# When a scatter is let go: threes of chunks, then quarters of a step, and a head in another order

## The chip, the cores and the metric

The kernel runs on one core of a Trainium2 chip. Its engines are TensorE (PE, with its weight loads shown apart as PEld), VectorE (DVE), ScalarE (ACT), GpSimd (POOL) and SyncE (SP); each works through its own instruction list in order, and they wait for each other through semaphores. The metric is the time of one execution on the device, in microseconds; shorter is better. The kernel before took 5031.5 us (median of 3 runs, 5031.15 to 5031.81).

## The reference

One layer of a graph network: 12,500 nodes with 128 features, 412,500 edges with 20 features, sorted by destination. `src` says to which node an edge's message is added, `dst` from which node it is taken.

```python
def ssp(x):
    return jax.nn.softplus(x) - LOG2
h = x @ W_in2f                              # here x is relu(layernorm(x))
Wij = ssp(f_ij @ W_f1 + b_f1) @ W_f2 + b_f2
Wij = Wij * rcut_ij[:, None]
x_ij = h[idx_j] * Wij                       # idx_j = dst
agg = jax.ops.segment_sum(x_ij, idx_i, num_segments=h.shape[0])   # idx_i = src
out = ssp(agg @ W_o1 + b_o1) @ W_o2 + b_o2
...
return x + out
```

## The kernel before

**Tiling.** The edges go in 806 chunks of 512 (`CH`), each of four tiles of 128 (`QT`). Four chunks make a group, whose inputs (f, rcut, window offsets) are loaded together. The nodes stand in 98 blocks of 128 and are prepared by quads of four blocks (`make_h`: layer norm, ReLU, product with W_in2f, split into bf16 parts, store to DRAM in the tables h, h_1, h_2, h_3). Quad 0 is `h[0]`, quad 1 is `h[1]`, and a third list, `aside`, makes the others from step 7 on.

**A chunk's way.** PE computes `z = f @ W_f1` for two chunks at a time (`hidden`, L710); ACT and DVE make the softplus of it (L719, L720, L722 and L742); PE computes the filter `v` (`value`, L834). Since the edges are sorted by destination, a chunk's gathered nodes lie in a window of 42 rows: SP loads it (`near`, L656), DVE builds a one-hot matrix (`window`, L818), PE picks the rows out (`pick`, L846), and ACT multiplies them by rcut (`picked`, hg, L856). DVE multiplies v by hg: that is the message `o` (L864).

**The sum by source.** Messages are not added at once. A counting sort on the fly gives each edge a slot: DVE compares block numbers (`blocks`, inb, L747), two PE matmuls add up the counts (`pass_on`, L799, and `rank`, L766; called "the counts" below), and DVE reads the rank out (`rank_end`, top, L771). POOL then writes the chunk's messages into slot tables in DRAM, with one indirect DMA per tile, so four scatters a chunk (`scatter`, L873). The slot tables belong to seven segments of chunks (`SEGS`: the first has 88 groups, chunks 0 to 351). When a segment is written, a `Collect` loads its slots back (m), compares (L932) and adds with matmuls (`add`, L953: acc and numbers). The first collect begins at chunk 352 + 17 = 369 (`DELAY` = 17). So the program has a stage A, chunks up to 368 without collects, and a stage B with them. In the end the output MLP and the residual follow.

**What sets the order.** The program's order is written out by hand: `step(k)` issues, for each engine, the work that belongs to step k, which is for PE v of chunk k+1, the pick of chunk k+2, the counts of a chunk some six ahead, z, and in stage B the collect's matmuls; each engine runs its instructions in that order. In the head, `HEAD = (0, 2, 4)` names steps with a special order.

**Pacing.** There are 16 message buffers (`BACK`). `behind` makes PE's v, pick and z of a chunk wait for scatters 16 chunks back (14 to 16 in effect). A scatter itself waits for the message (DVE), for the landing of the scatter eight before it (eight semaphores in turn), and, from chunk 24 (`PACED`) to the last twelve chunks, for PE: `scatter(k, kept["v"])`, called in `step(k)` right behind v of chunk k+1, lets chunk k-1 go, and its first scatter waits for that v. The other three follow it on POOL in order.

```python
if j >= PACED and k < NCH - PACED // 2   # else: no wait for PE
```

Of the kernel before, what the change touches and what calls it, by code (L numbers as in the profile page):

```python
# [17 lines left out]
P = 128  # L18
# [3 lines left out]
QT = CH // P  # L22
# [23 lines left out]
def gnn_kernel(  # L46
# [20 lines left out]
    nc = tc.nc  # L67
# [477 lines left out]
    with tc.tile_pool(name="edge", bufs=2) as edge, tc.tile_pool(  # L545
# [49 lines left out]
        def behind(inst, k, i):  # L595

            if k - BACK >= 0:
                tc.add_manual_dep(inst.ins, puts[(k - BACK) * QT + i],
                                  mybir.DependencyInfo(mybir.DependencyClass.Sync,
                                                       mybir.DependencyReason.DATA),  # L600
                                  reason="pace of the scatters")

        class Group:
# [101 lines left out]
            def hidden(self, c):  # L705

                z = psum.tile([P, 2, CH], F32, name="z")
                for k in range(2):
                    rows = slice(32 * (c + k), 32 * (c + k) + RBF)
                    mm = nc.tensor.matmul(z[:, k, :], wf1[rows, :], self.f[rows, :],  # L710
                                          start=True, stop=True)
                    if k == 1:
                        behind(mm, self.g * NCHUNK + c - LZ, 3)
                self.pair[c] = z

            def hidden_log(self, c):
# [36 lines left out]
            def rank(self, c):  # L753

                seg = self.seg
                if c == 0:
                    self.top = edge.tile([P, TG], F32, name="top")
                    self.slot = edge.tile([P, TG], I32, name="slot", bufs=8)
                k = self.g * NCHUNK + c
                if k > seg.c0:  # L760
                    self.pass_on()
                if k == seg.cleared and k > seg.c0:
                    used = self.used()
                    self.limit(6 * len(segs), ALU.is_gt, seg.low, used[:, :, :NBLK - 1])
                    self.limit(6 * len(segs) + 1, ALU.is_gt, seg.low_last, used[:, :, NBLK - 1:])
                nc.tensor.matmul(free, after, self.inb[c], start=k == seg.c0, stop=False,  # L766
                                 skip_group_check=True)
                kept["inb"] = self.inb[c]

            def rank_end(self, c):  # L770
# [58 lines left out]
            def value(self, c, v):  # L829

                r = self.pair[c // 2 * 2][:, c % 2, :]
                k = self.g * NCHUNK + c - 1
                for i in range(QT):
                    mm = nc.tensor.matmul(v[:, i, :], r[:, i * P:(i + 1) * P], wf2,  # L834
                                          start=False, stop=True, skip_group_check=True)
                    if i == 1:
                        behind(mm, k, k % 2)
                kept["v"] = mm
                return v

            def pick(self, c, at, ps):

                near = self.near.pop(c)
                k = self.g * NCHUNK + c - 2
                for i in range(QT):
                    mm = nc.tensor.matmul(ps[:, i, :], at[:, i * P:(i + 1) * P], near,  # L846
                                          start=i == 0, stop=i == QT - 1, skip_group_check=True)
                    if i == 1:
                        behind(mm, k, 2 + k % 2)

            def picked(self, c, ps):

# [11 lines left out]
                nc.vector.tensor_mul(o[:, :, :P], v, hg)  # L864
                self.o[c] = o

            def scatter(self, c, after=None):

                views = self.seg.views
                o = self.o.pop(c)  # L870
                for i in range(QT):
                    j = c * QT + i
                    put = nc.gpsimd.indirect_dma_start(  # L873
                        out=views[j % VIEWS],
                        out_offset=bass.IndirectOffsetOnAxis(ap=self.slot[:, j:j + 1], axis=0),
                        in_=o[:, i, :],
                        in_offset=None,
                    )
                    puts.append(put.ins.name)
                    if i == 0 and after is not None:  # L880
                        tc.add_manual_dep(
                            put.ins, after.ins.name,
                            mybir.DependencyInfo(mybir.DependencyClass.Sync,
                                                 mybir.DependencyReason.DATA),
                            reason="pace of TensorE")
                    if i == 0 and self.g * NCHUNK + c == self.seg.cleared:
                        for name in self.seg.clears:
                            tc.add_manual_dep(
                                put.ins, name,
                                mybir.DependencyInfo(mybir.DependencyClass.Sync,  # L890
                                                     mybir.DependencyReason.DATA),
                                reason="cleared slots")

        class Collect:
# [47 lines left out]
            def add(self, u):  # L942
                b0, nb, t0, nt = self.units[u]
                m, to = self.m.pop(u), self.to.pop(u)
                for j in range(nb * nt):
                    b, t = b0 + j // nt, t0 + j % nt
                    if b % QT == 0 and t == 0:
                        self.few = QT if "rest" in kept else 2
                    few = self.few
                    i = b % few  # L950
                    if i == 0 and t == 0:
                        self.acc[b // few] = self.room(b // few)
                    nc.tensor.matmul(self.acc[b // few][:, i, :], m[:, j, :P], to[:, j, :],  # L953
                                     start=t == 0, stop=t == self.seg.tiles(b) - 1)
# [42 lines left out]
        def of(k):  # L997
            return groups[k // NCHUNK], k % NCHUNK
# [14 lines left out]
        def pairs(make):  # L1013
            return lambda g, c: None if c % 2 else make(g, c)
# [34 lines left out]
        tops, ps = [], {}  # L1049
        waiting = []  # L1050
        LAG, PACED = 1, 24

        def step(k, units=()):

# [11 lines left out]
            def message(k):  # L1066
                g, c = of(k)
                g.message(c, vs.pop(k), hgs.pop(k))
                waiting.append(k)
                scatter(k)  # L1070

            def scatter(k, after=None):
                while waiting and (waiting[0] < PACED or k >= NCH - PACED // 2
                                   or after is not None and waiting[0] <= k - LAG):
                    j = waiting.pop(0)
                    g, c = of(j)
                    g.scatter(c, after if j >= PACED and k < NCH - PACED // 2 else None)

            if k in vs:
                message(k)  # L1080
            if not k:
                next(h[1])
            for r in tops:
                for _ in r:
                    pass
# [41 lines left out]
            for r in ready[-1:]:  # L1127
                next(r, None)
                tops.append(r)
            if k in HEAD:  # L1130
                part("end", made["log"] - 1, pairs(hidden_end))
            elif k != -1:
                part("log", min(k + LZ - 1, made["hidden"]), pairs(hidden_log))
            if k not in HEAD[:-1]:
                part("hidden", k + LZ, pairs(hidden))
            for c, u in units:
                if summed:
                    summed[0].add(summed[1])
                summed[:] = c, u

        zeros = {}
        units = {}
# [129 lines left out]
        with tc.manual_schedule():  # L1272
# [36 lines left out]
            for k in range(-3, max(NCH, max(units) + 1)):  # L1309
# [140 lines left out]
```

## Time and profile before

| | |
|---|---|
| median of 3 runs | 5031.5 us (5031.15 to 5031.81) |
| profiled execution, its own time | 5066.4 us |
| its span, first to last instruction | 5064.7 us |
| mean granted TensorE clock | 0.784 |
| instructions | 68,387 |
| scatters (L873) | 3224, mean 959 ns |
| moved by DMA | 858 MB, mean 169 GB/s |

The profile comes from one execution, which took 0.7% longer than the median. Busy times are by engine, in microseconds; a busy PE is not PE at its peak. The granted clock is the share of full speed that the chip gave TensorE. In a row of groups the last column is the idle time of the engine just before those instructions and what ended most of it: "issue" means that nothing in the profile was waited for, "remote" that a semaphore was waited for of which the profile shows no setter. In a row of a timeline the idle time before the instruction stands in brackets.

### The profile page before, as it was taken

How to read it: one execution, taken by the hardware profiler on the slowest of the kernel's cores; microseconds unless marked ns; L12 is line 12 of the kernel's file. 1: busy time of each engine (PE TensorE's matmuls, PEld its weight loads, DVE VectorE, ACT ScalarE, POOL GpSimd, SP SyncE). 2: the span in 40 equal slices, each digit the busy share in tenths (PEclk: the TensorE clock that was granted, in tenths of full speed). 3: DMA queues.
4: the chain of work that ended last, by engine and by line, in shares of the span. 5: the costliest groups of instructions: out<-in, count | busy, mean ns of one | idle time of the engine just before them, and what ended most of it. 6: DMA issues, size and time to landing. Idle time of an engine off the chain costs nothing. (4 is left out here: it accounts for less than half of the span.)

```text
span 5064.7 us, 68387 instructions
## 1 busy us (share of the span) xinstructions
PE 3601.4 (71%) x21594; PEld 2760.7 (55%) x21594; DVE 3149.0 (62%) x7192; ACT 2793.9 (55%) x5494; POOL 3135.5 (62%) x3298
## 2 busy tenths in 40 slices
PE   5666666566655565567777887887777787787778
PEld 3444444344433344356666666666666666666667
DVE  5565555555544454556666666666666676677767
ACT  5556566565555555555555555555555555555533
POOL 5566666666666666666666666666656666666553
PEclk7666666766666666679999888888988888888889
DMA  4555545445433334446657655567656765665658
GB/s 140 171 160 164 171 138 174 147 134 160 130 99 114 113 113 141 131 154 199 190 189 238 187 178 185 175 192 230 188 169 185 219 207 168 183 216 163 186 144 229
DMA packets 494767, 858.10 MB, mean 169 GB/s; under 512 B 141018, under 2 KB 276558, under 8 KB 494398
## 3 DMA queue, kind: packets, MB, share of 16 engines
q1 hardware_dynamic: 390798, 640.38, 42.3%
q0 software_dynamic: 103168, 213.15, 12.5%
q8 instruction: 174, 2.85, 0.2%
q14 instruction: 195, 1.60, 0.1%
q10 hardware_dynamic: 432, 0.13, 0.0%
HBM read 457.62 MB, written 395.69 MB: 168 GB/s over the span
## 5 line engine op out<-in xcount | busy, mean ns | idle before, releaser
L873 POOL DMA_INDIRECT slots<-o,slot x3224 | 3090.8, 959 | 1831.2 <-issue 808.9
L856 ACT ACTIVATE hg<-picked,rcut 128x128 f32<-128x128 f32 x3224 | 913.3, 366 | 1243.5 <-remote 356.7
L834 PEld LDWEIGHTS v<-wf,r 128*128 128x128 f32 x6448 | 1067.2, 247 | 324.2 <-issue 214.8
L834 PE MATMUL v<-wf,r 128*128 128x128 f32 x6448 | 1153.8, 335 | 73.4 <-issue 36.5
L864 DVE TENSOR_TENSOR o<-v,hg 128x512 f32<-128x512 f32 x806 | 553.0, 686 | 698.4 <-remote 207.0
L953 PEld LDWEIGHTS acc<-to,m 128*128 128x128 f32 x5660 | 782.1, 219 | 281.0 <-issue 144.0
L953 PE MATMUL acc<-to,m 128*128 128x128 f32 x5660 | 836.6, 308 | 117.1 <-DVE agg L987 45.2
L710 PE MATMUL z<-f,wf 20*128 20x512 f32 x1612 | 605.7, 826 | 355.7 <-issue 185.6
L771 DVE TENSOR_REDUCE top<-free 128x4 f32<-128x392 f32 x806 | 449.1, 557 | 602.2 <-remote 341.9
L932 DVE TENSOR_TENSOR to<-numbers,m 128x640 f32<-128x640 f32 (+3 forms) x793 | 630.4, 825 | 40.0 <-remote 12.0
L719 ACT ACTIVATE a<-z,bf 128x1024 f32<-128x1024 f32 x402 | 445.7, 1109 | 379.4 <-PE v L834 113.6
L747 DVE TENSOR_TENSOR inb<-numbers,blk 128x392 f16<-128x392 f32 x806 | 447.7, 556 | 297.3 <-PE picked L846 73.9
L846 PE MATMUL picked<-near,at 126*128 126x128 bf16 x3224 | 393.6, 248 | 330.2 <-issue 193.5
L799 PE MATMUL free<-inb,rest_of 128*128 128x392 f16 x806 | 318.1, 395 | 420.9 <-issue 277.2
L742 DVE SCALAR_TENSOR_TENSOR r<-z,nbf,a 128x1024 f32<-128x1024 f32 x402 | 513.5, 1277 | 127.9 <-ACT a L722 64.0
L826 ACT ACTIVATE v<-bf 128x512 f32<-128x512 f32 x806 | 486.6, 604 | 180.7 <-DVE o L864 72.5
L846 PEld LDWEIGHTS <-at 126*128 126x128 bf16 x3224 | 302.7, 114 | 389.7 <-issue 364.5
L953 PE MATMUL numbers<-to,m 128*128 128x128 f32 x2492 | 398.7, 324 | 121.0 <-DVE to L932 87.6
L953 PEld LDWEIGHTS numbers<-to,m 128*128 128x128 f32 x2492 | 367.5, 233 | 213.6 <-DVE to L932 136.6
L722 ACT ACTIVATE a<-a,half 128x1024 f32<-128x1024 f32 x402 | 461.5, 1148 | 13.1
L710 PEld LDWEIGHTS z<-f,wf 20*128 20x128 f32 x1612 | 152.4, 226 | 551.7 <-issue 303.0
L720 ACT ACTIVATE a<-a 128x1024 f32<-128x1024 f32 x402 | 424.9, 1057 | 12.8
(126 smaller groups left out, 1845.0 us busy)
## 6 DMA issues: line engine op xcount, KB each, us to landing
m<-slots SPq DMA_DIRECT2D x307, 387.0 KB
rel<-rel_d SPq DMA_DIRECT2D x202, 504.0 KB
m<-slots SPq DMA_DIRECT2D x278, 322.5 KB
f<-in_f_t SPq DMA_DIRECT2D x101, 512.0 KB
slots<-o,slot POOLq DMA_INDIRECT x3224
m<-slots SPq DMA_DIRECT2D x193, 258.0 KB
slots<-zero SPq DMA_DIRECT2D x96, 387.0 KB
slots<-zero SPq DMA_DIRECT2D x58, 516.0 KB
```

The lines of the kernel that those rows point to most:

```text
L710: mm = nc.tensor.matmul(z[:, k, :], wf1[rows, :], self.f[rows, :], start=True, stop=True)
L722: nc.scalar.activation(a, a, AF.Ln, bias=half, scale=0.5)
L742: nc.vector.scalar_tensor_tensor(r, z, nbf1, a, op0=ALU.max, op1=ALU.add)
L771: nc.vector.tensor_reduce(self.top[:, c * QT:(c + 1) * QT], free_v, axis=mybir.AxisListType.X, op=ALU.max)
L826: nc.scalar.activation(v, spread(bf12, QT), AF.Copy)
L834: mm = nc.tensor.matmul(v[:, i, :], r[:, i * P:(i + 1) * P], wf2, start=False, stop=True, skip_group_check=True)
L846: mm = nc.tensor.matmul(ps[:, i, :], at[:, i * P:(i + 1) * P], near, start=i == 0, stop=i == QT - 1, skip_group_check=True)
L856: nc.scalar.activation(hg[:, i, :], ps[:, i, :], AF.Copy, scale=self.rcut[:, j:j + 1])
L864: nc.vector.tensor_mul(o[:, :, :P], v, hg)
L873: put = nc.gpsimd.indirect_dma_start(out=views[j % VIEWS], out_offset=bass.IndirectOffsetOnAxis(ap=self.slot[:, j:j + 1], axis=0), in_=o[: ...
L932: nc.vector.tensor_tensor(to[:, :n, :], count_ps[:, None, :].to_broadcast([P, n, P]), m[:, :n, P:].to_broadcast([P, n, P]), op=ALU.is_equal)
L953: nc.tensor.matmul(self.acc[b // few][:, i, :], m[:, j, :P], to[:, j, :], start=t == 0, stop=t == self.seg.tiles(b) - 1)
```

## The change

Three parts.

1. `kept["mm"]` now holds the last matmul that was issued by any of z, counts, v, pick or the collect's add (before: `kept["v"]`, v alone). `scatter(k, point)` is called at four points of a step: behind v, behind the pick, behind the counts, and at the end. For chunks 24 to 368 it lets go twelve scatters (three chunks) at once, at the point "v", and only the first of the twelve waits for PE. From chunk 369 on (`LONE`) it lets go one scatter at each of the four points, and each waits for the last matmul issued there. Chunks under 24 and the last twelve steps are not paced, as before.
2. Quad 1 of the nodes, `h[1]`, was moved on in every step from 0 (in step 0 twice); now it begins in step 6.
3. In steps 1 and 3, z and v of the odd chunk k+2 are issued right behind the pick, ahead of the counts. Step 4 too now makes the next chunk's message early (`k <= HEAD[-1]`).

```diff
...
-                kept["v"] = mm
+                kept["mm"] = mm
...
                 nc.vector.tensor_mul(o[:, :, :P], v, hg)
                 self.o[c] = o
 
-            def scatter(self, c, after=None):
+            def scatter(self, c, tiles, after=None):
 
                 views = self.seg.views
-                o = self.o.pop(c)
-                for i in range(QT):
+                o = self.o[c] if tiles[-1] < QT - 1 else self.o.pop(c)
+                for i in tiles:
                     j = c * QT + i
                     put = nc.gpsimd.indirect_dma_start(
                         out=views[j % VIEWS],
...
                         in_offset=None,
                     )
                     puts.append(put.ins.name)
-                    if i == 0 and after is not None:
+                    if i == tiles[0] and after is not None:
                         tc.add_manual_dep(
                             put.ins, after.ins.name,
                             mybir.DependencyInfo(mybir.DependencyClass.Sync,
...
         tops, ps = [], {}
         waiting = []
         LAG, PACED = 1, 24
+        LONE = segs[0].c1 + DELAY
 
         def step(k, units=()):
 
...
             def message(k):
                 g, c = of(k)
                 g.message(c, vs.pop(k), hgs.pop(k))
-                waiting.append(k)
+                waiting.append((k, 0))
                 scatter(k)
 
-            def scatter(k, after=None):
-                while waiting and (waiting[0] < PACED or k >= NCH - PACED // 2
-                                   or after is not None and waiting[0] <= k - LAG):
-                    j = waiting.pop(0)
-                    g, c = of(j)
-                    g.scatter(c, after if j >= PACED and k < NCH - PACED // 2 else None)
+            def scatter(k, point=None):
+                while waiting:
+                    j, i = waiting[0]
+                    if j < PACED or k >= NCH - PACED // 2:
+                        n, after = QT - i, None
+                    else:
+                        where, n = ("v", 3 * QT) if j < LONE else ("each", 1)
+                        if point not in (("v", "pick", "rank", "end") if where == "each" else (where,)):
+                            return
+                        if j * QT + i + n > (k - LAG + 1) * QT:
+                            return
+                        after = kept["mm"]
+                    while n > 0:
+                        j, i = waiting.pop(0)
+                        g, c = of(j)
+                        e = min(QT, i + n)
+                        g.scatter(c, range(i, e), after)
+                        after = None
+                        n -= e - i
+                    if e < QT:
+                        waiting.insert(0, (j, e))
+                        return
 
             if k in vs:
                 message(k)
-            if not k:
-                next(h[1])
             for r in tops:
                 for _ in r:
                     pass
...
                 hgs[k + 1] = g.picked(c, ps.pop(k + 1))
                 if k + 1 not in vs:
                     vs[k + 1] = g.value(c, bs.pop(k + 1))
-                    scatter(k, kept["v"])
+                    scatter(k, "v")
             if k in HEAD:
                 part("log", k + LZ - 1, pairs(hidden_log))
             if has(k + 2):
...
                 if k + 2 not in ps:
                     ps[k + 2] = psum.tile([P, QT, P], F32, name="picked", tag="v", bufs=3)
                 g.pick(c, ats.pop(k + 2), ps[k + 2])
+                scatter(k, "pick")
                 if k + 2 > 0:
                     bs[k + 2] = g.bias(c)
+                if k in (1, 3):
+                    part("hidden", k + LZ, pairs(hidden))
+                    vs[k + 2] = g.value(c, bs.pop(k + 2))
             part("window", k + 3, window)
             if k not in HEAD:
                 part("end", min(k + LZ - 2, made.get("log", -1)), pairs(hidden_end))
...
                     keep()
             if k < NCH:
                 keep()
-            if 0 <= k < HEAD[-1]:
+            if 0 <= k <= HEAD[-1]:
                 message(k + 1)
             upto = max(made["rank"], min(k + LR, 2 * k + 3))
             ready = [ranks(j) for j in range(made["rank"] + 1, upto + 1)]
...
             for r in ready[-1:]:
                 next(r, None)
                 tops.append(r)
+            scatter(k, "rank")
             if k in HEAD:
                 part("end", made["log"] - 1, pairs(hidden_end))
             elif k != -1:
...
                 if summed:
                     summed[0].add(summed[1])
                 summed[:] = c, u
+            scatter(k, "end")
 
         zeros = {}
         units = {}
...
                 step(k, now)
 
                 if k >= 0:
-                    for m in h:
+                    for m in h[:1] if k <= HEAD[-1] + 1 else h:
                         next(m, None)
                 if k > NEXT - 3:
                     next(aside, None)
```

In stage A, POOL's list at chunk 107 (o are the messages, slots_116 the first segment's table; DMASW are landings of earlier scatters, the names in brackets are the engines waited for). Before, one chunk and the first row of the next:

```order
L873 DMA slots_116<-o,slot 206848x129 [waits DMASW4_49,DVE_49,PE_49]
L873 DMA slots_116<-o,slot 206848x129 [waits DMASW5_49]
L873 DMA slots_116<-o,slot 206848x129 [waits DMASW6_49]
L873 DMA slots_116<-o,slot 206848x129 [waits DMASW7_49]
L873 DMA slots_116<-o,slot 206848x129 [waits DMASW0_49,DVE_49,PE_49]
```

and now:

```order
L875 DMA slots_116<-o,slot 206848x129 [waits DMASW4_49,DVE_49]
L875 DMA slots_116<-o,slot 206848x129 [waits DMASW5_49]
L875 DMA slots_116<-o,slot 206848x129 [waits DMASW6_49]
L875 DMA slots_116<-o,slot 206848x129 [waits DMASW7_49]
L875 DMA slots_116<-o,slot 206848x129 [waits DMASW0_49,DVE_49,PE_49]
```

The wait for PE of the first row is gone; of three chunks only one, here the one in the last row, still has it, and that wait is for a v two chunks later than before.

In stage B, POOL's list at chunk 406. Before:

```order
L873 DMA slots_117<-o,slot 116992x129 [waits DMASW0_49,DVE_49,PE_49]
L873 DMA slots_117<-o,slot 116992x129 [waits DMASW1_49]
L873 DMA slots_117<-o,slot 116992x129 [waits DMASW2_49]
L873 DMA slots_117<-o,slot 116992x129 [waits DMASW3_49]
L873 DMA slots_117<-o,slot 116992x129 [waits DMASW4_49,DVE_49,PE_49]
```

and now:

```order
L875 DMA slots_117<-o,slot 116992x129 [waits DMASW0_49,DVE_49,PE_49]
L875 DMA slots_117<-o,slot 116992x129 [waits DMASW1_49,PE_49]
L875 DMA slots_117<-o,slot 116992x129 [waits DMASW2_49,PE_49]
L875 DMA slots_117<-o,slot 116992x129 [waits DMASW3_49,PE_49]
L875 DMA slots_117<-o,slot 116992x129 [waits DMASW4_49,DVE_49,PE_49]
```

Each of the four scatters of a chunk has a wait for PE, where only the first had one.

In the head, PE's list in step 1 (picked is chunk 3's pick, free the sum of the counts, xps the transposed nodes of quad 1, v that of chunk 3, which before is issued in step 2). Before, from the pick's last matmul on:

```order
L846 MATMUL picked<-near,at 128x128
L799 LDWEIGHTS rest_of
L799 MATMUL free<-inb,rest_of 128x392
L766 LDWEIGHTS after
L766 MATMUL free<-inb,after 128x392
L799 LDWEIGHTS rest_of
L799 MATMUL free<-inb,rest_of 128x392
L766 LDWEIGHTS after
L766 MATMUL free<-inb,after 128x392
L710 MATMUL z<-f,wf_62 128x512 x2
L367 MATMUL xps<-ident,xb 128x128 x4
L834 MATMUL v<-wf_63,r 128x128 x4
```

and now:

```order
L847 MATMUL picked<-near,at 128x128
L710 MATMUL z<-f,wf_62 128x512 x2
L835 MATMUL v<-wf_63,r 128x128 x4
L800 LDWEIGHTS rest_of
L800 MATMUL free<-inb,rest_of 128x392
L767 LDWEIGHTS after
L767 MATMUL free<-inb,after 128x392
L800 LDWEIGHTS rest_of
L800 MATMUL free<-inb,rest_of 128x392
L767 LDWEIGHTS after
L767 MATMUL free<-inb,after 128x392
```

z and the next v stand ahead of the counts, and quad 1's transposes are gone from this place.

SP's list at the same time (near are the windows of nodes, h_1 to h the tables that quad 1 is stored to). Before:

```order
L386 DMA h_1_89<-hb 128x3x384
L386 DMA h_2_90<-hb 128x4x384
L386 DMA h_3_91<-hb 128x2x384
L395 DMA h_87<-hb 128x4x384
L649 TENSOR_LOAD shift_130
L656 ISA
L656 DMA near<-h_1_89 126x128
```

and now:

```order
L656 DMA near<-h_1_89 126x128
L1335 DMA slots_116<-zero 96x1032 x2
L656 ISA
L656 DMA near<-h_1_89 126x128
L386 DMA h_1_89<-hb 128x3x384
L386 DMA h_2_90<-hb 128x4x384
L386 DMA h_3_91<-hb 128x2x384
L395 DMA h_87<-hb 128x4x384
```

The four stores of quad 1 stood ahead of the near loads of chunks 10 to 13; now they stand behind these four, of which the last two are shown.

More of the change, by code (lines that the diff above doesn't have):

```diff
@@ L765, in rank @@
                     self.limit(6 * len(segs) + 1, ALU.is_gt, seg.low_last, used[:, :, NBLK - 1:])
-                nc.tensor.matmul(free, after, self.inb[c], start=k == seg.c0, stop=False,
-                                 skip_group_check=True)
+                kept["mm"] = nc.tensor.matmul(free, after, self.inb[c], start=k == seg.c0,
+                                              stop=False, skip_group_check=True)
                 kept["inb"] = self.inb[c]
@@ L837, in value @@
                         behind(mm, k, k % 2)
-                kept["v"] = mm
+                kept["mm"] = mm
                 return v
@@ L849, in pick @@
                         behind(mm, k, 2 + k % 2)
+                kept["mm"] = mm
             def picked(self, c, ps):
@@ L952, in add @@
                         self.acc[b // few] = self.room(b // few)
-                    nc.tensor.matmul(self.acc[b // few][:, i, :], m[:, j, :P], to[:, j, :],
-                                     start=t == 0, stop=t == self.seg.tiles(b) - 1)
+                    kept["mm"] = nc.tensor.matmul(
+                        self.acc[b // few][:, i, :], m[:, j, :P], to[:, j, :],
+                        start=t == 0, stop=t == self.seg.tiles(b) - 1)
                     if t == self.seg.tiles(b) - 1 and (i == few - 1 or b == NBLK - 1):
```

## The prediction

> **What bounds the kernel now.** I read the page's busy table and clock row first, then the same by stage.
>
> ```profile
> PE 3601.4 (71%) x21594; PEld 2760.7 (55%) x21594; DVE 3149.0 (62%) x7192; ACT 2793.9 (55%) x5494; POOL 3135.5 (62%) x3298
> PEclk7666666766666666679999888888988888888889
> 200.00:2200.00 2000.00, 1212.92 (x5668) 819.65 (x5669) 1069.75 (x2721) 1166.28 (x2310) 1300.62 (x1356) 0.66 0.45 141
> 2300.00:4700.00 2400.00, 1904.26 (x12829) 1551.20 (x12826) 1638.34 (x3460) 1312.26 (x2584) 1493.86 (x1559) 0.87 0.63 193
> ...
> 200.00:2200.00 2000.00, 233.00 (x339) 0.66 0.45 141
> 2300.00:4700.00 2400.00, 267.29 (x390) 0.87 0.63 193
> ```
>
> The long rows give, after the length, busy time on PE, PEld, DVE, ACT and POOL, then granted clock, DMA share and GB/s; the two short ones are the messages (o, L864), one per chunk. So stage A (before the first collect, up to chunk 368) takes 2000/339 = 5.90 us a chunk, and stage B (with collects, from chunk 369) 2400/390 = 6.154. No engine is full in either: PE is busy 4.88 us of B's step. POOL is nearest to it, because its scatters go at a fixed beat. The groups and the waits say what it does when it isn't scattering:
>
> ```profile
> L873 POOL DMA_INDIRECT slots<-o,slot x3224 | 3090.8, 959 | 1831.2 <-issue 808.9
> ...
> POOL slots L873 <- PE free L766: 262.9, 135, 3.3
> POOL slots L873 <- remote: 202.9, 100, 3.3
> DVE top L771 <- remote: 341.9, 68, 8.5
> ```
>
> A scatter is 0.96 us and the next starts 0.30 later ("issue"), so a chunk's four take 5.05 us; the rest of a step POOL waits for PE. "Remote" marks waits with no releaser in the profile. The timeline shows what they are. First POOL, around one long run in A:
>
> ```profile
> 822.85 0.96 POOL L873 DMA_INDIRECT slots<-o,slot  x1 [2.54 <-PE free L766]
> ...
> 836.73 0.96 POOL L873 DMA_INDIRECT slots<-o,slot  x1 [0.30 <-issue]
> 840.30 0.97 POOL L873 DMA_INDIRECT slots<-o,slot  x1 [2.62 <-DVE at L818]
> ```
>
> Twelve scatters in a row, then a stop. The stretches of that run, and three of its instructions:
>
> ```profile
> 822.90:833.00 10.10, 8.07 (x35) 5.56 (x35) 6.18 (x15) 9.54 (x16) 7.67 (x9) 0.51 0.88 281
> 833.00:838.10 5.10, 0.81 (x10) 0.68 (x9) 0.00 (x0) 1.61 (x5) 3.77 (x4) 0.82 0.17 58
> 838.10:840.60 2.50, 0.69 (x2) 0.10 (x1) 1.31 (x3) 0.14 (x1) 0.30 (x1) 0.50 0.08 26
> ...
> 832.23 1.36 PE L834 MATMUL v<-wf,r 128*128 128x128 f32 x8
> 836.46 1.14 ACT L856 ACTIVATE hg<-picked,rcut 128x128 f32<-128x128 f32 x4 [3.66 <-remote]
> 839.29 0.57 DVE L771 TENSOR_REDUCE top<-free 128x4 f32<-128x392 f32 x1 [7.02 <-remote]
> ```
>
> For eight scatters all engines work; then, with POOL still scattering, PE, DVE and ACT stand almost still, and go on only some 2 us after POOL has stopped. DMA is nearly empty meanwhile (0.17), so it isn't bandwidth. My reading, which the traces suggest and don't prove: a long unbroken row of scatters holds up PE's progress or the news of it, and a pause of POOL lets it through. POOL's own wait is for PE's v, so each long row ends in a stop that it caused itself.
>
> In B it is the same with shorter rows, eight and then 2.21 us:
>
> ```profile
> 2540.86 0.96 POOL L873 DMA_INDIRECT slots<-o,slot  x1 [2.25 <-PE free L766]
> ...
> 2549.69 0.96 POOL L873 DMA_INDIRECT slots<-o,slot  x1 [0.30 <-issue]
> 2552.86 0.96 POOL L873 DMA_INDIRECT slots<-o,slot  x1 [2.21 <-PE picked L846]
> ```
>
> What a row of each length costs where it repeats (last: the scatters, POOL's busy time and count):
>
> ```profile
> 1680.00:1855.50 175.50, 20.55 (x30) 0.63 0.37 112
> 2480.70:2613.00 132.30, 84.29 (x88) 0.92 0.58 187
> 4726.50:4758.70 32.20, 19.14 (x20) 0.84 0.75 215
> 3127.30:3161.20 33.90, 19.19 (x20) 0.80 0.67 214
> ```
>
> Ten rows of twelve in A: 175.5/30 = 5.85 us a chunk. Eleven rows of eight in B: 132.3/22 = 6.014. Rows of four in B, five and five: 32.2/5 = 6.44 and 33.9/5 = 6.78.
>
> **The change, part by part.**
>
> *Threes, chunks 24 to 368 (345 chunks).* Two of three PE waits go, and the first of twelve scatters waits for v four chunks on, not two. Rows of twelve become the rule; today they stand among fours and eights (the mix costs 5.90). Queued behind the waiting scatter on POOL are only scatters, and PE needs those 14 chunks later, so nobody else waits. The repeated twelves price it: 5.85 - 5.90 = -0.05 x 345 = **-17 us**. The bounds: the cycle above, 840.30 - 822.85 = 17.45, is 5.82 a chunk (-28); 6.014, the eights of B, is the nearest dearer row (+39). I take -17, a row of thirty chunks in this very stage.
>
> *Quarters, chunk 369 to 793 (425 chunks).* Each scatter has its own PE wait: v of the step, pick, the last rank, the step's last matmul. A wait that is long satisfied is free:
>
> ```profile
> 2581.99 0.96 POOL L873 DMA_INDIRECT slots<-o,slot  x1 [0.30 <-PE free L766]
> ```
>
> The same 0.30 as without one, so 3 x 425 = 1275 more waits cost nothing by themselves. An unsatisfied one stops POOL within one scatter of PE's standing still, where now it runs to the chunk's end. Behind it are only scatters again. No row shows four waits a chunk. From below: POOL back to back, 5.05 (-1.10 x 425 = -468). From above: the worst fours, 6.78 (+266). I take the eights, 6.014: a row of scatters stops where PE is seen to stop, at about eight, and the fours between go since a chunk no longer runs in one piece. (6.014 - 6.154) x 425 = **-60 us**.
>
> *The head.* Quad 1's normalisation and h leave steps 0 to 5 for 6 to 11, and in steps 1 and 3 z and the odd chunk's v pass ahead of the counts on PE; chunk 5's message comes within step 4.
>
> ```profile
> 22.20:59.00 36.80, 26.12 (x121) 17.15 (x120) 26.05 (x72) 22.84 (x46) 20.32 (x21) 0.75 0.45 147
> 59.00:101.80 42.80, 21.11 (x110) 15.06 (x108) 19.68 (x55) 22.45 (x44) 25.86 (x27) 0.66 0.44 135
> ...
> L362 DVE TENSOR_SCALAR xb<-xb,mv,rs 128x128 f32<-128x128 f32 x8 | 2.2, 358 | 0.1
> L346 DVE BATCH_NORM_STATS2 st<-xb 128x6 f32<-128x128 f32 x8 | 2.1, 266 | 0.0
> L347 DVE BATCH_NORM_AGGREGATE mv<-st 128x2 f32<-128x6 f32 x8 | 1.5, 182 | 0.3
> 41.53 0.69 DVE L864 TENSOR_TENSOR o<-v,hg 128x512 f32<-128x512 f32 x1 [2.98 <-PE v L834]
> ```
>
> Half of those eights are quad 1's: 4 x (358 + 266 + 182) ns = 3.2 us of DVE leave 22.2 to 59 (26.05 busy of 36.8) and land in 59 to 101.8 (19.68 of 42.8), where 23 us of idle DVE hide them. DVE waited 2.98 us for one odd chunk's v. Both edits together are worth from 0 to 3.2 + 2.98 = 6.2; what can be late next is the near load of the first chunks that need quad 1, since on SP its four h stores now stand behind the near loads of chunks 10 to 13 (up to 2.98 the other way, by the same kind of wait). I take **-5**.
>
> Sum: -17 - 60 - 5 = -82 us of an execution that spans 5064.7 us and took 5066.4. The median of the runs is 5031.5, 0.7% less; 82 x 0.993 is 81, so 5031.5 - 81 = **4950 us**.
>
> **The clock.** In the long cycle the clock shown is 0.51 in the work before PE's stop and 0.50 after it, and A's mean is 0.66. The Trainium skill, "TensorE: Matmul & The Clock Gate", Part 1, says that PE falls to half its clock after an idle window of about 3.4 us; that speaks against rows of twelve, and the stop of 833 to 840.6 agrees. The rival below prices it from rows.
>
> **The rivals.**
> 1. *Quarters become lockstep* (slower). POOL asks PE four times a chunk, the answers come late each time, and pauses are added to the stops instead of replacing them: the step is that of the fours, 6.44: +0.29 x 425 = +122, with -22 from the rest 5131 us; with 6.78, 5275. For it: fours are the dearest rows of B, and they are those in which POOL asks most often. Against: they lie where PE has more to do (0.84 and 0.80 of clock, 0.75 and 0.67 DMA against 0.58), so they may be the consequence. It decides once B's step passes 6.154 + 22/425 = 6.21.
> 2. *Same idle, other places*: PE needs so much POOL pause per chunk, however dealt out; A 5.90, B 6.154, the head alone: 5027 us. For it: twelves and eights cost about the same per chunk. Against: the mix in B is 0.14 dearer than eights alone.
> 3. *PE stops half as often*: POOL's shorter pauses are enough. In 2540.9 to 2551.0, before a stop, PE was busy for 9.12 of 10.1 us:
>
> ```profile
> 2540.90:2551.00 10.10, 9.12 (x60) 7.76 (x61) 7.22 (x14) 3.29 (x11) 7.62 (x8) 0.83 0.56 173
> ```
>
> At that share B's 4.88 us would take 5.40; half way there from 6.154 is 5.78: -0.37 x 425 = -159, with the others 4850 us; all the way 4692.
> 4. *Half clock throughout A* (slower): PE's 1212.92/339 = 3.58 us a chunk at 0.66 would be 4.72 at 0.50; three of them, with the 7.6 us of standing (1.5 of it busy), 20.3 a cycle, 6.76 a chunk: +0.86 x 345 = +297, in all about 5263. Against: the repeated twelves run at 0.63 and 5.85. By the page's rule every cycle does so begin cold; the trace agrees, and has its price inside the 5.85.
> 5. *The quarter waits never bite*: POOL is so far behind PE that all are satisfied; B stays at 6.154, and A and head give 5010 us.
>
> **How the numbers follow.** Forecast 0.42, rivals 1 to 5: 0.28, 0.08, 0.13, 0.04, 0.05. Runs here lie within 0.01%, and 0.2% is about what can be told from no change. Faster: 0.42 + 0.13 + 0.05 = 0.60. Same: 0.08. Slower: 0.28 + 0.04 = 0.32. The range runs from 4830 (rival 3 a little over its half) to 5120 (rival 1 a little short of the 6.44); what it leaves out is about half of rival 1 (0.12), rival 4 and a few hundredths of rival 3. The forecast's own range, with A between -28 and +39 and B between -0.05 and -0.25 a step, is 4880 to 5040.
>
> **What would show it.** Threes: between 200 and 2200 us POOL goes in rows of twelve and nothing else, each followed by 2 to 3 us, with 342 messages instead of 339. A step over 5.95 there makes the term wrong. Quarters: in B no row of scatters beyond about eight, pauses spread inside the chunk, step near 6.0; a step above 6.21 with pauses of over a microsecond inside chunks is rival 1, one below 5.85 with PE's share near 0.9 is rival 3. Head: chunk 6's o (59.0 us now) and chunk 12's (101.8) some 5 us earlier. The prediction is wrong as a whole if PE's standing still isn't caused by the row of scatters; then the waits move POOL and nothing else.

## The result

The changed kernel took 5052.8 us (median of 6 runs, 5042.4 to 5058.7), the kernel before 5030.9 beside it (6 runs). The ratio is 1.0046, interval 1.0033 to 1.0058: slower by 0.46%, some 22 us. Forecast were 4950 us and a gain. The time lies inside the range, the direction is wrong.

The profiled execution after took 5051.1 us (span 5049.3). That of before was an unusually long one, 5066.4 against 5021.7 to 5031.8 in the six runs, so the two traces compared as wholes point the wrong way; they are read here by stages, and the sizes come from the runs. Messages (o, now L866) by stage, in the trace after:

```profile
200.00:2200.00 2000.00, 231.04 (x336) 0.65 0.44 138
2300.00:4700.00 2400.00, 272.42 (x396) 0.88 0.64 196
```

Stage A made 336 chunks where it made 339 (342 were forecast): 5.95 us a chunk. Stage B made 396 where it made 390: 6.06. Since the trace of before is a long one, its 390 is low; the experiments below have 394 for the same pacing.

POOL's timeline in A has rows of twelve and nothing else, as forecast. Most are followed by 2.5 us of pause, but some by far more:

```profile
1041.50 0.96 POOL L875 DMA_INDIRECT slots<-o,slot  x1 [2.59 <-PE v L835]
...
1055.42 0.96 POOL L875 DMA_INDIRECT slots<-o,slot  x1 [0.30 <-issue]
1063.91 0.96 POOL L875 DMA_INDIRECT slots<-o,slot  x1 [7.54 <-PE v L835]
```

A pause here is idle time of more than 1 us between two scatters. Of the 112 pauses between 190 and 2200 us, 17 are over 3.2 us long and hold 88.5 us; before, of 79 pauses behind rows of twelve there were 3, with 10.6 us.

In B the rows are shorter and of many lengths, mostly three to eight, and the pauses between them 1.0 to 2.5 us:

```profile
2540.27 0.96 POOL L875 DMA_INDIRECT slots<-o,slot  x1 [2.06 <-PE picked L847]
...
2549.12 0.96 POOL L875 DMA_INDIRECT slots<-o,slot  x1 [0.30 <-issue]
2552.59 0.96 POOL L875 DMA_INDIRECT slots<-o,slot  x1 [2.50 <-DVE inb L748]
...
2557.65 0.96 POOL L875 DMA_INDIRECT slots<-o,slot  x1 [0.30 <-issue]
2559.95 0.96 POOL L875 DMA_INDIRECT slots<-o,slot  x1 [1.34 <-PE numbers L955]
...
2562.48 0.96 POOL L875 DMA_INDIRECT slots<-o,slot  x1 [0.30 <-issue]
2564.43 0.96 POOL L875 DMA_INDIRECT slots<-o,slot  x1 [1.00 <-remote]
```

In the head, chunk 6's message comes 3.4 us later than before (59.04), now waiting for ACT:

```profile
62.41 0.69 DVE L866 TENSOR_TENSOR o<-v,hg 128x512 f32<-128x512 f32 x1 [3.00 <-ACT a L720]
```

Chunk 12's comes at 99.3 us, 2.5 us earlier than before.

### The profile page after: what moved, and what is told of

It reads as the page before. It is cut to its first block, busy times and chain, and to the rows that moved or that the text cites. A ratio compares the mean times of both kernels' runs of the same rounds, so it can differ in the third digit from the quotient of the medians.

```text
span 5049.3 us, 69659 instructions
## 1 busy us (share of the span) xinstructions
PE 3619.0 (72%) x21594; PEld 2772.8 (55%) x21594; DVE 3154.3 (62%) x7192; ACT 2789.2 (55%) x5494; POOL 3145.9 (62%) x3298
## 5 line engine op out<-in xcount | busy, mean ns | idle before, releaser
L835 PE MATMUL v<-wf,r 128*128 128x128 f32 x6448 | 1169.8, 337 | 121.9 <-issue 64.2
L866 DVE TENSOR_TENSOR o<-v,hg 128x512 f32<-128x512 f32 x806 | 554.2, 688 | 801.9 <-remote 310.1
L720 ACT ACTIVATE a<-z,bf 128x1024 f32<-128x1024 f32 x402 | 446.4, 1110 | 270.1 <-remote 81.8
```

## The experiments

Each kernel below is the changed one with the lines shown. "Head as before" means that part 2 and part 3 of the change are undone:

```diff
+            if not k:
+                next(h[1])
...
-                if k in (1, 3):
-                    part("hidden", k + LZ, pairs(hidden))
-                    vs[k + 2] = g.value(c, bs.pop(k + 2))
...
-            if 0 <= k <= HEAD[-1]:
+            if 0 <= k < HEAD[-1]:
...
-                    for m in h[:1] if k <= HEAD[-1] + 1 else h:
+                    for m in h:
```

With that and `("v", QT)` for all chunks, the instruction lists of all engines are those of the kernel before.

The runs fell on several chips, and the kernel before itself took from 4201 to 5078 us on them. A ratio is always to runs of the kernel before on the same chip, made together with them; a difference in microseconds is that of the two medians. Where an expectation says that a part "pays", it means that this part bears the loss.

**The parts alone, on a chip other than that of the result.** Threes alone, quarters alone (both with the head as before), and the head alone:

```diff
-                        where, n = ("v", 3 * QT) if j < LONE else ("each", 1)
+                        where, n = ("v", 3 * QT) if j < LONE else ("v", QT)      # threes
+                        where, n = ("v", QT) if j < LONE else ("each", 1)        # quarters
+                        where, n = ("v", QT)                                     # head, which keeps parts 2 and 3
```

> Only the threes of chunks 24 to 368; quarters and head as before. Theory 'threes pay' (a fixed row of twelve makes PE stand still in every cycle): stage A at 6.0 us a chunk or a little less, 15 to 40 us slower than the kernel before (5046 to 5071). Theory 'quarters pay': no difference that can be told (5021 to 5041), rows of twelve in A at 5.85 to 5.90.

> Only the quarters from chunk 369; A and head as before. Theory 'threes pay': 0 to 40 us faster (4991 to 5031), stage B at 6.05 to 6.10 us a chunk, as in the profile after. Theory 'quarters pay': 15 to 40 us slower (5046 to 5071), B above 6.15.

> Only the head: quad 1 in steps 6 to 11, z and the odd chunk's v ahead of the counts. Both theories: 5 to 10 us faster (5021 to 5026), with chunk 24's message at 170 us instead of 177.5. If the head itself pays, it is slower, and the gain at chunk 24 is given back later.

The kernel before, unchanged, for a second trace:

> The kernel before once more, for a second trace: its profiled execution took 5066 us, 35 more than the median. If that execution was an unusual one, its stages A and B come out cheaper here, by some 35 us together (A near 5.85, B near 6.11 a chunk); if a profile costs this kernel time, the second trace is as long as the first.

None of the theories fits: on this chip the kernel before took 4201.2 us, 830 less than on the chip of the result, and the parts were level with it: threes 1.0000 (0.9991 to 1.0009), quarters 0.9998 (0.9989 to 1.0007), head 0.9996 (0.9987 to 1.0005), the kernel before 1.0001. The trace of the kernel before on this chip shows why. Its stages (the whole-core windows, then the messages):

```profile
200.00:1700.00 1500.00, 1034.46 (x5101) 702.71 (x5100) 955.23 (x2417) 1042.80 (x2076) 1138.29 (x1187) 0.71 0.54 167
1900.00:3900.00 2000.00, 1747.60 (x13007) 1449.99 (x13006) 1648.19 (x3507) 1317.81 (x2613) 1517.02 (x1582) 0.92 0.77 234
...
200.00:1700.00 1500.00, 208.21 (x304) 0.71 0.54 167
1900.00:3900.00 2000.00, 270.80 (x396) 0.92 0.77 234
```

B takes 2000/396 = 5.05 us a chunk, just POOL's four scatters back to back. So does POOL in A (1187 scatters in 1500 us, 5.05 for four), where the messages run a little ahead of it (4.93) while the 16 buffers fill. POOL's group and the longest wait:

```profile
L873 POOL DMA_INDIRECT slots<-o,slot x3224 | 3093.8, 960 | 1011.9 <-issue 722.8 <-DMA slots<-o,slot 59.1 <-DVE o L864 31.4
...
DVE o L863 <- DMA slots<-o,slot: 671.1, 286, 7.7
```

The 3224 scatters are busy for 3094 of the 4199 us, and most of the rest is the 0.30 between two of them. Of the other engines' waits DVE's for a free message buffer is the longest, that is a wait for POOL. No wait of the list is put down to "remote". So the scatters are equally long, and all the instructions are the same, but PE doesn't stand still behind rows of scatters, although POOL's row there hardly ever breaks. Where POOL is always behind, no wait for PE bites, and how scatters are let go made no difference that can be told.

**The change again, on another chip.**

> The changed kernel once more, beside the kernel before on one chip. Theory 'POOL's beat' (where PE does not stand still, four scatters a chunk at 1.26 us set the pace and PE is always ahead of every wait): no difference that can be told beside 4201 us, as with each part alone. Theory 'standing still': if the kernel before takes about 5031 us here, as it did first, 10 to 30 us slower than it, and the trace shows rows of twelve in A.

There the kernel before took 5064.4 us and the change 5137.5: 1.0132 (1.0092 to 1.0172). So the loss is not peculiar to the chip of the result, but its size is: 22 us there, 73 here, where 10 to 30 had been expected for a chip like that of the result.

**The parts again, and sixes.** The three kernels above where PE does stand still (the kernel before 5025.5 us), and in place of the threes, with the head as before, rows twice as long. The record gives this chip the same number as that of the run before, but there the kernel before took 5058.7 to 5084.5 us and here 5013.2 to 5028.5. Either it is not the same chip or its speed had changed; why is open.

```diff
-                        where, n = ("v", 3 * QT) if j < LONE else ("each", 1)
+                        where, n = ("v", 6 * QT) if j < LONE else ("v", QT)
```

> The threes alone again, for a chip on which PE stands still (the kernel before above 5000 us). Theory 'threes pay': 20 to 60 us slower, A at 5.95 to 6.1 us a chunk, in rows of twelve with pauses of about 3 us. Theory 'quarters pay': within 10 us. On a chip where the kernel before takes about 4200 us all four of this call but the sixes are within 0.1%.

> The quarters alone again. Theory 'threes pay': 0 to 40 us faster, B at 6.05 to 6.1 us a chunk. Theory 'quarters pay': 20 to 60 us slower.

> The head alone again: 5 to 10 us faster by both theories, chunk 24's message 5 to 8 us earlier.

> Six chunks at once in A (rows of 24 scatters, 30 us), B and head as before. Theory 'rows make PE stand still': PE works for about the first 8 scatters and then stands to the row's end, so six steps of about 4 us must follow in the pause: A at 7 us a chunk or more, in all some 400 us slower. Theory 'rows are harmless, PE only needs the same pause per chunk': A at 5.5 to 6.0, within 100 us. On a chip without standing still POOL loses up to 345/6 pauses at most: 4200 to 4300 us.

| alone | time, us | ratio (interval) | difference, us |
|---|---|---|---|
| threes | 5073.5 | 1.0103 (1.0087 to 1.0120) | +48 |
| quarters | 5007.5 | 0.9967 (0.9952 to 0.9981) | -18 |
| head | 5025.6 | 0.9999 (0.9989 to 1.0008) | 0 |
| sixes | 5602.2 | 1.1155 (1.1132 to 1.1177) | +577 |

The loss is the threes'. 48 - 18 + 0 is 30 us, near the 22 of the chip of the result. The head missed the 5 to 10 us that were expected of it: chunk 24's message came at 176.4 us, against 175.4 and 177.4 in the traces of quarters alone and threes alone, which have the head as before. The 577 us of the sixes are more than the 400 expected, and far from the 100 of harmless rows: they show that it is the row that holds PE up where PE stands still. One of their rows, 24 scatters from 1026.6 to 1056.6, and the pause behind it:

```profile
1026.60:1036.70 10.10, 7.29 (x46) 5.77 (x45) 5.03 (x13) 7.51 (x15) 7.66 (x8) 0.83 0.59 163
1036.70:1056.60 19.90, 3.70 (x14) 2.21 (x14) 3.25 (x6) 2.74 (x7) 15.31 (x16) 0.59 0.20 69
1056.60:1073.90 17.30, 11.63 (x50) 8.19 (x50) 10.80 (x24) 13.10 (x26) 0.02 (x1) 0.50 0.50 168
...
200.00:2200.00 2000.00, 183.71 (x267) 0.62 0.36 112
```

During the first eight scatters PE is busy for 7.3 of 10.1 us, during the other sixteen for 3.7 of 19.9, and the steps that are missing are made up in the pause, which is 17.35 us long. The row is a usual one: over the 42 such rows between 250 and 2150 us PE is busy for 6.8 and 4.4 us. A takes 2000/267 = 7.49 us a chunk, as the theory of standing still had it.

But then a twelve behind which PE stands for five microseconds should cost what the repeated twelves cost, 5.85. Where the threes lose is seen by splitting A: messages in 200 to 1250 and 1300 to 2200 us with threes alone, then with the head alone (whose pacing is that of before), on the same chip:

```profile
200.00:1250.00 1050.00, 118.90 (x173) 0.66 0.49 152
1300.00:2200.00 900.00, 107.31 (x156) 0.65 0.39 123
```

```profile
200.00:1250.00 1050.00, 123.41 (x180) 0.67 0.50 158
1300.00:2200.00 900.00, 106.72 (x155) 0.65 0.39 122
2300.00:4700.00 2400.00, 270.44 (x394) 0.88 0.63 195
```

6.07 against 5.83 in the first part, 5.77 against 5.81 in the second. With threes the median pause is 2.56 us, hardly longer than the 2.44 with the head alone; but of 17 pauses above 3.2 us (89 us in all) 15 lie before 1250 us. The loss can also be followed chunk by chunk, in one trace of each, against quarters alone, which has the same head and the old pacing in A. Threes alone is 10 us later at chunk 24's first scatter, 45 at chunk 222's and 44 at chunk 368's. The first 10 us lie in the first row of three chunks, which waits for the v four chunks on (first quarters alone, then threes alone); in the two runs further down with a quad every six steps, threes against single chunks, this is 2 us:

```profile
183.04 0.96 POOL L875 DMA_INDIRECT slots<-o,slot  x1 [9.86 <-DVE row_of L687]
```

```profile
193.13 0.96 POOL L875 DMA_INDIRECT slots<-o,slot  x1 [17.97 <-PE v L835]
```

The stretch up to 1250 us is where the side list `aside` makes the node quads 2 to 24, one begun every nine steps. This gave a new theory, "quads in the pause", against "threes as such".

**Threes late, quarters everywhere, and both.** All with the head as before:

```diff
-                        where, n = ("v", 3 * QT) if j < LONE else ("each", 1)
+                        where, n = ("v", 3 * QT if 222 <= j < LONE else QT)                          # threes late
+                        where, n = ("each", 1)                                                       # quarters everywhere
+                        where, n = ("v", 3 * QT if 222 <= j else QT) if j < LONE else ("each", 1)    # late threes, quarters
```

> Threes only for chunks 222 to 368, where the node quads of the side list are done; before that one chunk at a time, B and head as before. In the run with all threes the long pauses (over 3.2 us, 17 of 113, 89 us together) lie between 210 and 1245 us but for two. Theory 'quads in the pause' (a long pause comes where a quad's part falls into PE's standing still): within 10 us of the kernel before, 5 us faster at best. Theory 'threes as such' (POOL may not take one or two chunks when only these are ready): 147/345 of the 48 us, some 20 us slower.

> Quarters from chunk 24 on, no threes, head as before. Theory 'quarters spread the pauses' (as in B, -0.05 us a chunk): 30 to 40 us faster, A at 5.80. Rival 'A's rows of twelve are its best': A at 5.95 or more, as B's mixed rows are, and the whole 0 to 30 us slower than before.

> Threes for chunks 222 to 368 and quarters from 369, head as before: the sum of the two, so 15 to 28 us faster by 'quads in the pause', 0 by 'threes as such'.

The kernel before took 5078.1 us here. Threes late: 1.0008 (0.9992 to 1.0024), 5 us above it and not to be told from it, where "threes as such" had 20. Late threes with quarters: 0.9972 (0.9956 to 0.9989), -14 us: about what the quarters bring alone (-18). Quarters everywhere: 0.9953 (0.9940 to 0.9967), -18 us. That is the lowest ratio of all the runs, but its interval overlaps those of late threes with quarters and of quarters alone (0.9967), so it can't be called better than these. Of the 30 to 40 us forecast for it 18 came. Its trace and, below it, that of late threes with quarters, whose first part is paced as before:

```profile
200.00:1250.00 1050.00, 122.45 (x178) 0.66 0.50 157
1300.00:2200.00 900.00, 106.04 (x154) 0.63 0.39 122
2300.00:4700.00 2400.00, 268.96 (x391) 0.88 0.63 193
```

```profile
200.00:1250.00 1050.00, 121.76 (x177) 0.68 0.49 155
1300.00:2200.00 900.00, 105.09 (x153) 0.64 0.39 121
2300.00:4700.00 2400.00, 268.37 (x390) 0.87 0.64 193
```

One message more in each part, B included, where both are paced alike. So A's rows, now of one to thirteen scatters, cost nothing there, and the 0.03 us a chunk that they seem to bring (1050/177 - 1050/178) is no more than one execution of each can show. A stands at 1050/178 = 5.90 and 900/154 = 5.84 us a chunk, not at the 5.80 looked for.

**Threes early, and the quads moved.** Threes only before chunk 222; threes in all of A with a node quad begun every six steps; and that spacing alone:

```diff
+                        where, n = ("v", 3 * QT if j < 222 else QT)       # threes early
...
-                if i % 9 == 0 and 2 + i // 9 < NQ:                        # quads every six steps, in side()
-                    quads.append(make_h(2 + i // 9, psum))
+                if i % 6 == 0 and 2 + i // 6 < NQ:
+                    quads.append(make_h(2 + i // 6, psum))
```

> Threes only for chunks 24 to 221, where the node quads are made; after that one chunk at a time. Theory 'quads in the pause': nearly all of the 48 us, 35 to 50 slower. Theory 'threes as such' (the late run was cheap by chance): 198/345 of it, 20 to 30.

> Threes in all of A, but a new node quad is begun every 6 steps instead of 9, so the last is done near chunk 150 (about 940 us) and not near 210 (1250 us). Theory 'quads in the pause': the pauses over 3.5 us end at about 940 us too, and their number stays near 17 or falls with the number of cycles that hold a quad's part. Rival 'the early stretch' (something else that ends at 1250 us): they go on to 1250 us.

> The control: a node quad every 6 steps, all else as before. By both theories within 15 us of the kernel before; what it differs by is taken off the run above.

With the kernel before at 5067.2 us, early threes took 1.0127 (1.0098 to 1.0156), +63 us, more than the 35 to 50 expected; so the cost lies in the early chunks, as far as runs on two chips can be set side by side. Threes with quads every six steps took 1.0161 (1.0131 to 1.0190), +80; the control 1.0018 (1.0001 to 1.0034), +11, so 69 are left, near the 63 of the early threes. And the long pauses moved with the quads. POOL's rows behind a pause, and the span of the quads' L377, in that run:

```profile
791.06 0.95 POOL L875 DMA_INDIRECT slots<-o,slot  x1 [2.82 <-remote]
812.97 0.96 POOL L875 DMA_INDIRECT slots<-o,slot  x1 [6.95 <-PE v L835]
830.47 0.96 POOL L875 DMA_INDIRECT slots<-o,slot  x1 [2.65 <-remote]
852.30 0.95 POOL L875 DMA_INDIRECT slots<-o,slot  x1 [6.99 <-PE v L835]
...
L377 DVE TENSOR_TENSOR hps<-hps,hb x20: 432/699/700, 219.3 to 960.4; 128x512 f32<-128x512 f32 x19, 128x256 f32<-128x256 f32 x1
```

Six steps are two cycles of threes, and now every second pause is 7 us long. Of 19 pauses over 3.5 us the last but one ends at 931 us, the quads at 960, and only one stands alone later (its end is at 1112). What happens in the cycle of 830.47 to 852.30 is in the timeline:

```profile
838.52 1.85 PE L373 MATMUL hps<-win,xT 128*128 128x128 f32 x8
...
847.63 0.60 ACT L375 ACTIVATE hb<-hps 128x512 bf16<-128x512 f32 x1 [6.09 <-remote]
848.13 1.13 ACT L858 ACTIVATE hg<-picked,rcut 128x128 f32<-128x128 f32 x4
...
849.29 0.60 ACT L827 ACTIVATE v<-bf 128x512 f32<-128x512 f32 x1
...
849.95 2.08 PE L835 MATMUL v<-wf,r 128*128 128x128 f32 x8 [5.91 <-ACT v L827]
```

The quad's product hps is done at 840.4, but then the stand begins (the time in which PE, ACT and DVE hardly work), and ACT gets on with it (hb, L375) only at 847.6, two microseconds after POOL's row. Behind hb in ACT's order stand a chunk's hg and the bias of a v, and that v, at 849.95, is the one for which POOL is waiting: the third since the row began. In the cycle before, without such a part, the third came at 821.71, while POOL was still scattering (its row went from 812.97 to 827.8). PE's v of the two rows:

```profile
813.56 1.91 PE L835 MATMUL v<-wf,r 128*128 128x128 f32 x8
818.47 1.16 PE L835 MATMUL v<-wf,r 128*128 128x128 f32 x8
821.71 2.08 PE L835 MATMUL v<-wf,r 128*128 128x128 f32 x8 [0.16 <-issue]
835.74 1.91 PE L835 MATMUL v<-wf,r 128*128 128x128 f32 x8
840.21 1.06 PE L835 MATMUL v<-wf,r 128*128 128x128 f32 x8
849.95 2.08 PE L835 MATMUL v<-wf,r 128*128 128x128 f32 x8 [5.91 <-ACT v L827]
```

So such a cycle costs 4.3 us more, 6.95 against 2.65. How much of that is hb's place in ACT's order and how much the quad's other work ahead of it was not tested apart.

The traces say how far this explains the long pauses. From 190 to 2200 us of this run hb starts inside a pause 18 times; these 18 pauses are long, and the only long one without an hb is that of 1112 us. With threes alone and a quad every nine steps it starts in a pause 8 times, and all 8 are long (5.3 us or more); three more of the 17 long pauses hold another quad instruction, and six hold none. One of these six, 7.3 us before chunk 168's scatters, comes back with 7.3 to 7.8 us in all five traces with threes there (it is the 7.54 shown in the result and the one at 1112 us); what it waits for is open. With the old pacing hb starts in a pause too, 8 times with the head alone and 4 with quarters alone, and none of these is over 3.2 us. So the quads cost what they do only together with the threes.

## Why the prediction was wrong

*Threes: -17 forecast, +48 measured* (+63 for their early half on another chip). This is the step that failed, and it turned the sign. "The repeated twelves price it" took 175 us from 1680 us on for the whole stage. The rows do become twelves and the ordinary cycle is the one priced: 12 x 1.263 us less 0.30 and 2.56 of pause make 17.4, 5.81 a chunk. But those twelves stand behind the last node quad. Between 200 and 1250 us 15 of 58 pauses are long, 5.2 us on average, which is 2.6 more than the usual 2.56: some 39 us, which with the 10 us of the first row (2 in another pair of runs) is about the size of the loss. Before, POOL was not bound to three chunks: when PE was one or two ahead it took a row of four or eight. That these rows, read as a dearer mix, were the slack is the reading that fits; it is not shown by itself. Where the priced twelves stand, behind the quads, threes alone ran at 5.77 us a chunk against 5.81 for the old pacing, so there the price held, in one execution of each; the run with late threes (+5, not to be told from 0) confirms no gain. The upper bound, +39, was also too low: it was taken from rows of eight, in a stage without quads.

*Quarters: -60 forecast, -18 measured.* Direction right, size a third. "A row of scatters stops where PE is seen to stop, at about eight, and the fours between go" is the part that failed: the rows do end at eight or sooner, but the fours did not go; most rows came to be of three to six with pauses of 1.0 to 2.2 us. Stage B of quarters alone:

```profile
2300.00:4700.00 2400.00, 272.93 (x397) 0.89 0.64 197
```

POOL's idle time a chunk went from 6.09 - 5.05 = 1.04 us (head alone) to 6.05 - 5.05 = 1.00 (quarters alone: 2400/397). That is the second rival's "same idle, other places", with a few hundredths gained. That satisfied waits cost nothing held: the gap stayed 0.30.

*Head: -5 forecast, 0 measured.* Chunk 6's message, looked for 5 us earlier, came 3.4 us later and waited for ACT's softplus (3.00 us, L720) instead; that this wait ate the 3.2 us taken from DVE is argued, not tested. The risk named, the near loads, doesn't show in the waits.

*The sum.* The terms give 4950. The forecast's own range, though, adds up from its terms (with the head at -5) to 4892 to 5044, not to 4880 to 5040. That the time fell into the wide range is luck as far as the threes go: the range was set by rivals about the quarters.

*The rivals.* Lockstep (1) did not come: B got cheaper. Half clock throughout A (4) did not: 0.65 against 0.66. PE stopping half as often (3) did not on these chips. The result, slower by 22 us, had a cause that no rival held. The sum of parts, 48 - 18 + 0 = +30, agrees with it in sign and, the chips differing as they do, in size.

*The reading behind it all* was right where it was tested, and less general than it was put: sixes show that a long row of scatters makes PE stand still, on those chips. On one chip nothing of it is seen, with the same program. "DMA is nearly empty meanwhile (0.17), so it isn't bandwidth" was read from one stand. In two others of the same trace the DMA engines were full:

```profile
502.70:507.70 5.00, 0.00 (x0) 0.00 (x0) 0.00 (x0) 1.74 (x5) 3.84 (x4) 0.75 0.98 242
...
927.60:932.70 5.10, 0.38 (x4) 0.26 (x4) 0.00 (x0) 0.89 (x2) 3.81 (x4) 0.92 0.94 266
```

So a stand comes with full and with nearly empty DMA engines; the empty ones show that bandwidth is not needed for it, the full ones leave open whether it adds to some. What differs between the chips isn't known, and neither is what it is that PE waits for in the stand; the profile calls it "remote".

## What to carry to other kernels

A stretch of repeated cycles prices only work that is like it: before it is multiplied by a whole stage, look which side lists run in the rest and whether their parts can fall into the cycle's pause. A coarser release takes away the freedom to go on with less, and that costs at the irregular places, not in the median; look at the longest pauses, not the usual one. And where an engine waits for reasons that the profile can't name, see whether another chip shows them, before a schedule is tuned around them.

## What the runs showed of the hardware

The same kernel took 4201 us on one chip and 5025 to 5078 in the other sets of runs. On the first no wait is put down to "remote" and POOL's four scatters (5.05 us a chunk) are the bound; on the others PE, ACT and DVE do little from about the ninth of a row of indirect scatters on, until some 2 us after a row of twelve and 3 to 4 us after a row of 24. In the rows shown PE is busy for 0.8 of 5.1 us in the last four scatters of twelve and for 3.7 of 19.9 in the last sixteen of 24, with the DMA engines at 0.17 and 0.20 of their time. On the first chip each part of the change alone was within 0.04% of the kernel before.
